# Slot attention and an FP8-weight FFN on one core: unsplit float32 products in the whole first unit, and other places for the norm blocks' transposes

## The chip, the cores and the metric

The kernel runs on one core of a Trainium2 chip. The metric is the device time of one execution in microseconds, here the median of three runs. The core's engines run their own instruction streams side by side and wait for each other by semaphores: PE (TensorE, matrix products and transposes), DVE (VectorE), ACT (ScalarE), POOL (GpSimd), and SP, which issues most DMAs.

## The reference, cut to what matters

Four sequences of 512 tokens with 512 features go through two residual blocks:

```python
x = x + attn(layernorm(x), Wq, Wk, Wv, Wg, Ws, Wo, g_norm_weight)
x = x + ffn(layernorm(x), gate_w, up_w, down_w, gate_scale, up_scale, down_scale)

# attn, 16 heads, DK = M = 64, DV = 128
q, k, v = heads(x @ Wq) * DK**-0.5, heads(x @ Wk), heads(x @ Wv)
s = clip(heads(x @ Ws), -32, 32)
z = cumlogsumexp(s); p = exp(s - z); g = exp(z_before - z)
hk = hk * g + k * p;  ok = q . hk          # over time
pv = softmax(ok)
hv = hv * g + p * v;  o = pv . hv          # over time
o = o * rsqrt(mean(o**2) + eps) * g_norm_weight * silu(x @ Wg)
return o @ Wo

# ffn: weights rounded to float8_e4m3, silu(gate) * up, then down
```

The two recurrences are computed in blocks of 128 tokens: products inside a block under a triangular mask, and states summed over the earlier blocks.

## The kernel before, in words

**Units.** `attention(g, b, before, load)` handles two heads (group g of 8) of one sequence b. The 32 units run in the order (0,0), (0,1), (1,0), (1,1) ... (7,1), then the same with b = 2, 3 (L1013); the text counts them as unit 0 to unit 31. A unit with even g projects values for two groups. Each unit also finishes the one before it (`before`): scaling, turning, gating and projecting its output. After the units comes the FFN over the four sequences in 12 chunks of the hidden size (L1076 on).

**Split products.** PE multiplies float32 operands that were prepared as float32r. A matrix or an activation is split into three parts, hi, lo and a mixed one (L238 to L250 for weights, `parts` L336 for activations: two DVE instructions and one of ACT). A projection is then eight products into one PSUM buffer ("main", four hi, then four lo) and four into another ("mixed"); ACT evacuates the first and DVE subtracts the second (L469 to L489, values L510 to L526). The PSUM pool `proj` has three buffers. In unit 0, the projections s, k and q take unsplit operands (L492 to L503): four products of float32 with `raw` weights and with `whole`, the unsplit norm of sequence 0, which lies in a buffer of tag "v".

**Order.** The schedule is written out by hand: each engine executes in the order in which the code emits (L998). Side work stands in a list `work` of named entries. `other()` takes `pace` entries from its front and emits them, `need(key)` takes entries from the front until none of that name is left. `pace` is 2 in a unit that starts with entries in `steps`, else 1 (L1054). `load_matrix(nm, g, True)` queues the split of a weight matrix: one entry for the first hi piece on ACT, then for each piece of 512 columns an entry with the next hi on ACT and two DVE instructions ("rest"), which at a matrix's end also issues the copy of the split to DRAM on SP; s, k and q have one piece, g and o two, v four. Raw weights come through two buffers; `fetch()` issues the next raw load once a buffer's split is done. In the first 16 units the matrices are split, in the later 16 units the splits are read back from DRAM and `work` holds the rounding of the FFN weights ("round", entries of two DVE instructions).

**Norm blocks.** `layernorm(b, which)` queues for sequence b four `measure` entries (three DVE instructions and a power on POOL) and the first `normalise` entries. It returns a function that puts four entries into `steps`; `next_step()` emits one: four PE transposes of a block of 128 tokens into a PSUM bank (one of three in turn), ACT's copy of the hi part, and a queue entry "xs_b" with the block's `parts`. The bank is `held`: the next use of it emits these parts first. Norms are transposed in unit 0 (for b=1), unit 15 (for b=2), unit 16 (for b=3), unit 31 (for the FFN of b=0) and in the FFN.

**A unit's order on PE.** Slots s, keys k, queries q, turns of e and k; values in four blocks (even g) with the previous unit's output turned between them, or that output's turn alone (odd g); query_key (a), the two gates, slot_scores (ok), value_states (sv), softmax (okn), the previous unit's output projection o in four blocks, slot_weights (w), weight_slot (b), read_out (ov). `softmax` on DVE is a maximum and a subtraction; `softmax_exp` is on ACT.

Of the kernel before, what the change touches and what calls it, by code (L numbers as in the profile page):

```python
# [37 lines left out]
F32 = mybir.dt.float32  # L38
# [6 lines left out]
P = 128  # L45
# [4 lines left out]
def kernel(  # L50
# [116 lines left out]
    def other(count=None):  # L167
        for _ in range(count or pace[0]):
            if work:
                work.pop(0)[1]()  # L170

    def need(key):

        while any(name == key for name, _ in work):
            other(1)
# [46 lines left out]

    def load_matrix(nm, g, first):
        words = CHUNKS[nm] * MATRICES[nm][1]
        w = one.tile([P, 3, words], F32R, tag=f"w_{nm}", name=f"w_{nm}_{g}")
        wt[nm] = w
        if not first:
            nc.sync.dma_start(w.bitcast(F32), split[nm, g])
            return
        scale = QSCALE if nm == "q" else 1.0  # L230
        pieces = words // 512

        def source(n):

            per = min(pieces, RAW // 512)
            return raw[nm, g][n // per][:, n % per * 512 : (n % per + 1) * 512]

        def high(n):  # L238
            nc.scalar.mul(w[:, 0, n * 512 : (n + 1) * 512], source(n), UNDER * scale)

        def rest(n):
            cols = slice(n * 512, (n + 1) * 512)
            hi, lo = w[:, 0, cols].bitcast(F32), w[:, 1, cols].bitcast(F32)
            if scale == 1.0:
                nc.vector.tensor_tensor(w[:, 1, cols], source(n), hi, ALU.subtract)  # L245
            else:
                nc.vector.scalar_tensor_tensor(
                    w[:, 1, cols], source(n), scale, hi, ALU.mult, ALU.subtract
                )
            nc.vector.scalar_tensor_tensor(w[:, 2, cols], hi, DELTA, lo, ALU.mult, ALU.subtract)  # L250
            if (n + 1) * 512 % RAW == 0 or n + 1 == pieces:
                if g > 0 or nm in "vo":
                    fetch()
            if n + 1 == pieces:
                split[nm, g] = dram.tile(
                    [P, 3, words], F32, tag=f"split_{nm}_{g}", name=f"split_{nm}_{g}"
                )
                nc.sync.dma_start(split[nm, g], w.bitcast(F32))

        def step(n):  # L260

            if n + 1 < pieces:
                high(n + 1)
            rest(n)

        work.append((nm, lambda: high(0)))
        work.extend((nm, lambda n=n: step(n)) for n in range(pieces))
# [21 lines left out]
    def layernorm(b, which, n_bank=None):  # L289
# [59 lines left out]
        if start:  # L349
            for n in range(NT):  # L350
                measure(n)
                if n > 0:
                    normalise(n - 1)
                    transposes(n - 1)
            normalise(NT - 1)
            transposes(NT - 1)
            work.extend((f"xs_{b}", lambda n=n: parts(n)) for n in range(NT))
            return None
        key = f"xn{which}_{b}_"
        todo = [(key + "m", lambda n=n: measure(n)) for n in range(NT)]  # L360
        todo.insert(2, (key + "0", lambda: normalise(0)))
        todo.insert(4, (key + "1", lambda: normalise(1)))
        at = max([i + 1 for i, (name, _) in enumerate(work) if name in ("xs_0", "v", "g")], default=0)
        work[at:at] = todo

        def step(n):
# [96 lines left out]
    class Projection:  # L463
# [5 lines left out]
        def main(self, to):  # L469
# [8 lines left out]
            self.to = to  # L478
            nc.scalar.mul(to, self.p, 1.0 + DELTA)  # L479

        def mixed(self):

            self.m = ps3.tile([P, T], F32, tag="proj", name=f"ps_{self.name}_m")
            for c in range(KC):
                nc.tensor.matmul(  # L485
                    self.m, products(self.nm, c, self.col0, 2), xs[self.b][2][:, c, :],
                    start=(c == 0), stop=(c == KC - 1),
                )
            nc.vector.tensor_tensor(self.to, self.to, self.m, ALU.subtract)  # L489

    def project(nm, b, name, to, between=None):
        if name == f"{nm}_0_0":  # L492
            p = ps3.tile([P, T], F32, tag="proj", name=f"ps_{name}")
            for c in range(KC):
                nc.tensor.matmul(
                    p, raw[nm, 0][0][:, c * P : (c + 1) * P], whole[0][:, c, :],
                    start=(c == 0), stop=(c == KC - 1),
                )
            other({"s": NT + 2, "k": 1, "q": 3}[nm])
            nc.scalar.mul(to, p, QSCALE if nm == "q" else 1.0)  # L500
            if between:
                between()
            return  # L503
        p = Projection(nm, b, 0, name)
        p.main(to)
        if between:
            between()
        p.mixed()

    def project_v(b, n, name, to):  # L510

        p = ps3.tile([P, 2 * HV], F32, tag="proj", name=f"ps_{name}")
        m = ps3.tile([P, 2 * HV], F32, tag="proj", name=f"ps_{name}_m")
        for dst, which in ((p, (0, 1)), (m, (2,))):
            for i in which:
                for c in range(KC):
                    nc.tensor.matmul(  # L517
                        dst,
                        xs[b][i][:, c, n * P : (n + 1) * P],
                        wt["v"][:, i, c * 2 * HV : (c + 1) * 2 * HV],  # L520
                        start=(i == which[0] and c == 0),
                        stop=(i == which[-1] and c == KC - 1),
                    )
            if dst is p:
                nc.scalar.mul(to, p, 1.0 + DELTA)  # L525
        nc.vector.tensor_tensor(to, to, m, ALU.subtract)  # L526
# [48 lines left out]
    class Heads:  # L575
# [168 lines left out]
        def gate_main(self, h):  # L744
            self.sg.append(one.tile([P, T], F32, tag=f"sg{h}", name=f"sg_{self.u}_{h}"))
            self.pg = Projection("g", self.b, h * DV, f"g_{self.u}_{h}")
            self.pg.main(self.sg[h])

        def gate_mixed(self, h):
            self.pg.mixed()  # L750
# [54 lines left out]
    def attention(g, b, before, load):  # L805
# [7 lines left out]
                before.project_output(n)  # L813
                before.add_output(n)

        if b or g:
            need(f"xs_{b}")
            need("s")
        X.slots()
        load("s")  # L820
        if before:
            before.scale_output()
        if b or g:
            need("k")

        def running_sum():
# [4 lines left out]

        X.keys(running_sum)
        load("k")
        if b or g:
            need("q")
        X.queries(other if even and before else None)
        load("q")
        X.turn_e()
        if even:
            X.turn_k()  # L840
            need(f"xs_{b}")
            need("v")
            X.values(0)
            if before:
                before.turn_output(0)
# [1 line left out]
            X.inverse()  # L847
            X.values(1)
            other()
            if before:  # L850
                before.high_output(0)
                before.split_output(0)
                before.turn_output(1)
# [6 lines left out]
            next_step()  # L860
            X.values(3)
            other()
        else:
            before.turn_output(0)
            X.turn_k()
# [5 lines left out]
            before.split_output(0)  # L871
            before.split_output(1)
            X.inverse()
            next_step()
        need("g")
        X.gate_main(0)
        X.gate_mixed(0)
        if even or steps:
            other()
            next_step()  # L880
        X.gate_main(1)
        X.gate_mixed(1)
        load("g")
        if even:
            load("v")
        X.gate_silu(0)
        X.gate_silu(1)
        exp_and_log()
        X.slot_scores()
        X.value_states()  # L890
        if even:
            other()
        if before:
            next_step()
        X.softmax()
        if not before:
            next_step()
        if not even:
            other()
        if before:  # L900
            need("o")
            before.project_output(0)
# [1 line left out]
        if before:  # L904
            before.add_output(0)
            before.project_output(1)
        X.slot_weights()
        if before:
            before.add_output(1)
# [88 lines left out]
    with tc.manual_schedule(engines=EVERY):  # L998
# [3 lines left out]
            (nc.scalar if n % 2 else nc.sync).dma_start(x1[0][:, n, :], blocks[:, n, :])  # L1002
        exp_and_log()
        fetch_first()
        layernorm(0, 1)
        for nm in "vgskqo":
            load_matrix(nm, 0, True)
        load_tokens(1, x)
        for b in range(2):
# [6 lines left out]
        for i, (g, b) in enumerate(units):  # L1016
            last = i + 1 == len(units)

            def load(nm):
                after = (i + 1 + 2 * (nm == "v")) // 2 * 2  # L1020
                if b == B - 1 and after == len(units):
                    for c, tag in enumerate(PLACES):
                        if tag == f"w_{nm}":
# [46 lines left out]
                load_ffn(c)  # L1070

        assert not work and not steps
        before.scale_output()
        before.scale_other()
        prev, kept = None, []
        for b in range(B):  # L1076
            need(f"xs_{b}")
            for c in range(NFC):
                if c > 1:
                    other(2)  # L1080
                h = ffn_hidden(b, c)
                if b == 0 and 0 < c < 3:
                    before.turn_output(c - 1, 2)
                    before.high_output(c - 1)
                    before.split_output(c - 1)
# [2 lines left out]
                    before.add_output(c - 3)  # L1088
                if c == 1 and b + 1 < B:
                    load_tokens(b + 1, stream, *((two, "v"), (one, "tokens"), (one, "y"))[b])  # L1090
                    layernorm(b + 1, 2, 2)()
                if prev is not None:
                    pb, pc, parts = prev
# [56 lines left out]
```

## Time and profile before

| | |
|---|---|
| median of 3 runs (lowest, highest) | 1534.4 us (1533.82, 1536.49) |
| the profiled execution, its span | 1534.67 us, 1532.9 us |
| mean granted TensorE clock | 0.991 |
| busy: PE, PEld | 1466.4 us (96%), 1182.0 us (77%) |
| busy: DVE, ACT, POOL | 1112.2 us (73%), 705.8 us (46%), 191.1 us (12%) |
| moved by DMA | 212.53 MB, mean 139 GB/s |

PE is the matrix engine's product stream, PEld its weight loads, which run beside it. Busy time is the time in which an engine executes an instruction; the rest it waits or is issued nothing. In timelines a row is: start in us from the span's start, duration in us, engine, line, operation, written tile <- read tiles, shapes, count, and in brackets the idle time before it and what ended it. The first groups of the page for the unsplit products (line 495), in us busy and mean ns of one record:

```profile
L495 PE MATMUL ps_s<-xn_whole,raw_sk 128*128 128x512 f32 x8 | 6.1, 938 | 0.7 <-ACT xn_whole L329 0.7
L495 PE MATMUL ps_k<-xn_whole,raw_sk 128*128 128x512 f32 x8 | 3.6, 592 | 0.0
L495 PE MATMUL ps_q<-xn_whole,raw_q 128*128 128x512 f32 x8 | 3.6, 592 | 0.0
```

Each has eight records for the four products of the code. The first of them ran at the clock of the start, before the full clock was granted at 17.9 us.

### The profile page before, as it was taken

The page shows a single profiled execution, that of the slowest core. Times are in us where ns is not written, and L with a number is a line of the kernel's source. Part 1 is how long each engine was busy: PE and PEld are TensorE (multiplying, and loading weights), DVE is VectorE, ACT ScalarE, POOL GpSimd, SP SyncE. Part 2 cuts the span into 40 slices and gives each one's busy share as a digit, 9 for nine tenths or more (in the row PEclk, how much of TensorE's full clock was granted, in tenths as well). Part 3 has the DMA queues.
Part 4 walks back from the last instruction along what each step waited for, and adds up shares of the span by engine and source line. Part 5 has one row for each costly group of instructions (what it writes and reads, how often), then busy time and mean ns, then how long its engine had stood idle before and what let it go on. Part 6 is the DMA issues. An engine that isn't in the chain of part 4 may idle for free.

```text
span 1532.9 us, 23073 instructions
## 1 busy us (share of the span) xinstructions
PE 1466.4 (96%) x9077; PEld 1182.0 (77%) x9077; DVE 1112.2 (73%) x1974; ACT 705.8 (46%) x1214; POOL 191.1 (12%) x204
## 2 busy tenths in 40 slices
PE   7799899999999999889999999999999989999998
PEld 4678688778877888677777778777777768787886
DVE  7678767877888788777888888888888754445333
ACT  4455445564565555444554454445444543222221
POOL 1011110111111111110111111111111111000000
PEclk9899999999999999999999999999999999999999
DMA  8146545575555564436564746575565452101000
GB/s 311 67 137 180 178 111 164 167 221 153 144 187 183 151 220 131 103 68 224 123 185 104 246 109 175 137 231 138 156 183 168 133 162 28 55 1 56 0 28 28
DMA packets 80716, 212.53 MB, mean 139 GB/s; under 512 B 6152, under 2 KB 34848, under 8 KB 75424
## 3 DMA queue, kind: packets, MB, share of 16 engines
q1 hardware_dynamic: 61792, 176.96, 31.6%
q0 software_dynamic: 18528, 33.58, 15.5%
q8 instruction: 71, 1.16, 0.3%
q10 hardware_dynamic: 288, 0.52, 0.1%
q14 instruction: 37, 0.30, 0.1%
HBM read 107.23 MB, written 108.00 MB: 140 GB/s over the span
## 4 chain that ended last, share of the span: by engine, by line
PE 78%; DVE 14%; ACT 4%; issue 2%; DMA 1%; POOL 0%; SPq 0%; DVEq 0%; ACTq 0%; POOLq 0%
PE ps_v L517 8%; PE ps_o L784 7%; PE ps_fu L929 5%; PE ps_fg L929 4%; PE ps_g L474 4%; PE ps_ov L714 4%; PE ps_v_m L517 4%; PE ps_o_m L784 3%; PE ps_q L474 3%; PE ps_g_m L485 3%; PE ps_s L474 3%; PE ps_k L474 3%; PE ps_b L544 2%; PE ps_a L544 2%; PE ps_fd L973 2%; PE ps_fe L973 2%
## 5 line engine op out<-in xcount | busy, mean ns | idle before, releaser
L800 POOL DMA_DIRECT2D stream<-y x128 | 110.9, 869 | 921.2 <-DVE y L799 916.2
L784 PE MATMUL ps_o<-w_o,oT 128*128 128x512 f32 x512 | 151.2, 416 | 2.3 <-DVE w_o L245 2.1
L794 ACT ACTIVATE y<-ps_o 128x512 f32<-128x512 f32 x128 | 76.3, 596 | 126.5 <-PE ps_o L784 125.4
L517 PE MATMUL ps_v<-w_v,xs 128*128 128x512 f32 x512 | 132.9, 401 | 0.0
L474 PE MATMUL ps_g<-xs,w_g 128*128 128x512 f32 x512 | 129.1, 394 | 0.0
L950 DVE SCALAR_TENSOR_TENSOR h<-ps_fu,scol,act 128x512 f32<-128x512 f32 x48 | 36.0, 750 | 105.2 <-PE ps_fu L929 102.6
L474 PEld LDWEIGHTS ps_g<-xs,w_g 128*128 128x128 f32 x512 | 94.6, 188 | 20.7
L517 PEld LDWEIGHTS ps_v<-w_v,xs 128*128 128x128 f32 x512 | 92.3, 188 | 20.4
L784 PEld LDWEIGHTS ps_o<-w_o,oT 128*128 128x128 f32 x512 | 90.5, 191 | 21.8 <-DVE w_o L245 2.7
L774 ACT ACTIVATE oT<-oT 128x512 fp32r<-128x512 f32 x64 | 40.5, 633 | 133.1 <-DVE oT L771 133.1
L799 DVE TENSOR_TENSOR y<-y,ps_o_m 128x512 f32<-128x512 f32 x128 | 87.2, 681 | 16.4 <-ACT y L794 8.0
L929 PE MATMUL ps_fg<-xs,wf 128*128 128x512 f32 x384 | 97.1, 395 | 0.0
L929 PE MATMUL ps_fu<-xs,wf 128*128 128x512 f32 x384 | 95.1, 390 | 1.2 <-ACT act L947 1.2
L929 PEld LDWEIGHTS ps_fu<-xs,wf 128*128 128x128 f32 x384 | 72.0, 188 | 16.7 <-ACT act L947 1.6
L784 PE MATMUL ps_o_m<-w_o,oT 128*128 128x512 f32 x256 | 81.4, 399 | 1.8 <-ACT y L794 1.7
L929 PEld LDWEIGHTS ps_fg<-xs,wf 128*128 128x128 f32 x384 | 71.7, 189 | 14.7
L526 DVE TENSOR_TENSOR v<-v,ps_v_m 128x512 f32<-128x512 f32 x64 | 43.9, 685 | 47.5 <-PE ps_v_m L517 41.4
L956 ACT CAST both<-h 128x512 fp32r<-128x512 f32 x48 | 29.8, 620 | 105.2 <-DVE h L950 105.2
L485 PE MATMUL ps_g_m<-xs,w_g 128*128 128x512 f32 x256 | 70.6, 398 | 4.3 <-ACT sg L479 4.3
L489 DVE TENSOR_TENSOR sg<-sg,ps_g_m 128x512 f32<-128x512 f32 x64 | 43.9, 686 | 41.6 <-PE ps_g_m L485 38.2
L525 ACT ACTIVATE v<-ps_v 128x512 f32<-128x512 f32 x64 | 37.9, 592 | 76.6 <-PE ps_v L517 76.6
L729 POOL TENSOR_TENSOR rs<-rs,mhalf 128x8 f32<-128x8 f32 x32 | 58.6, 1830 | 87.5 <-DVE rs L726 82.1
(159 smaller groups left out, 3218.3 us busy)
## 6 DMA issues: line engine op xcount, KB each, us to landing
stream<-y POOLq DMA_DIRECT2D x128, 256.0 KB, 5.3
split_v<-w_v SPq DMA_DIRECT2D x4, 3072.0 KB, 12.0
split_g<-w_g SPq DMA_DIRECT2D x8, 1536.0 KB, 8.2
split_o<-w_o SPq DMA_DIRECT2D x8, 1536.0 KB, 6.1
w_v<-split_v SPq DMA_DIRECT2D x4, 3072.0 KB, 15.2
w_g<-split_g SPq DMA_DIRECT2D x8, 1536.0 KB, 6.7
w_o<-split_o SPq DMA_DIRECT2D x8, 1536.0 KB, 9.5
rounded<-qw SPq DMA_DIRECT2D x36, 256.0 KB, 4.1
```

The lines of the kernel that those rows point to most:

```text
L474: nc.tensor.matmul(self.p, products(self.nm, c, self.col0, i), xs[self.b][i][:, c, :], start=(i == 0 and c == 0), stop=(i == 1 and c == KC ...
L485: nc.tensor.matmul(self.m, products(self.nm, c, self.col0, 2), xs[self.b][2][:, c, :], start=(c == 0), stop=(c == KC - 1),)
L517: nc.tensor.matmul(dst, xs[b][i][:, c, n * P : (n + 1) * P], wt["v"][:, i, c * 2 * HV : (c + 1) * 2 * HV], start=(i == which[0] and c == 0 ...
L544: nc.tensor.matmul(pa[h][:, n, :], lT[rows, cols], rT[rows, cols], start=True, stop=True)
L714: nc.tensor.matmul(po[h][:, n, :], self.bb[h][:, n, :], both_v[self.b][:, n, self.v0 + h * DV : self.v0 + (h + 1) * DV], start=False, stop ...
L729: nc.gpsimd.tensor_tensor(rs, rs, mhalf.rearrange("p (h n) -> p h n", h=HG), ALU.pow)
L784: nc.tensor.matmul(dst, self.oT[:, i, h, n * P : (n + 1) * P], wt["o"][:, i, h * D : (h + 1) * D], start=(i == which[0] and h == 0), stop= ...
L794: nc.scalar.mul(y, p, 1.0 + DELTA)
L799: nc.vector.tensor_tensor(y, y, m, ALU.subtract)
L800: nc.gpsimd.dma_start(stream[self.b][n * P : (n + 1) * P, :], y, accum_op=ALU.add)
L929: nc.tensor.matmul(pp, w[:, c * P : (c + 1) * P], xs[b][k][:, c, :], start=(c == 0 and k == 0), stop=(c == KC - 1 and k == 1),)
L973: nc.tensor.matmul(sums[n], parts[k][:, n * P : (n + 1) * P], fw[c][2], start=(c == 0 and k == 0), stop=(c == NFC - 1 and k == 1),)
```

## The change

In unit 0 all projections take unsplit operands: values from `whole` and the raw v pieces, gates from the raw g. The two gates move from before slot_scores to both sides of softmax. The splits of v, g and o of group 0, and the four `parts` of sequence 0's norm, are queued late in unit 0 instead of at the start; s, k and q are split first. The split tile `w` is allocated when its first piece is emitted. In all units with a predecessor, `other()` of even g moves from before softmax to behind it, where odd g has it. Where `steps` holds norm blocks, their transposes are emitted at other places: in odd units after slots and after keys (`early_step`), in even units after values 1, 2 and 3 and between the gates. The measures of a later norm are queued behind "v", "g" and "q" entries instead of "xs_0", "v" and "g". In the FFN the last unit's output is scaled after the first hidden block, and the next sequence's norm is queued at chunk 2 instead of 1.

```diff
     def load_matrix(nm, g, first):
         words = CHUNKS[nm] * MATRICES[nm][1]
-        w = one.tile([P, 3, words], F32R, tag=f"w_{nm}", name=f"w_{nm}_{g}")
-        wt[nm] = w
+
+        def begin():
+            wt[nm] = one.tile([P, 3, words], F32R, tag=f"w_{nm}", name=f"w_{nm}_{g}")
+
         if not first:
-            nc.sync.dma_start(w.bitcast(F32), split[nm, g])
+            begin()
+            nc.sync.dma_start(wt[nm].bitcast(F32), split[nm, g])
             return
...
         def high(n):
+            if n == 0:
+                begin()
+            w = wt[nm]
...
-            work.extend((f"xs_{b}", lambda n=n: parts(n)) for n in range(NT))
-            return None
+            return [(f"xs_{b}", lambda n=n: parts(n)) for n in range(NT)]
...
-        at = max([i + 1 for i, (name, _) in enumerate(work) if name in ("xs_0", "v", "g")], default=0)
+        at = max([i + 1 for i, (name, _) in enumerate(work) if name in ("v", "g", "q")], default=0)
...
+        def whole(self):
+
+            p = ps3.tile([P, T], F32, tag="proj", name=f"ps_{self.name}")
+            width = MATRICES[self.nm][1]
+            for c in range(KC):
+                at = c * width + self.col0
+                nc.tensor.matmul(
+                    p, raw[self.nm, 0][0][:, at : at + P], whole[0][:, c, :],
+                    start=(c == 0), stop=(c == KC - 1),
+                )
+            return p
...
-            other({"s": NT + 2, "k": 1, "q": 3}[nm])
+            p = Projection(nm, b, 0, name).whole()
+            other({"s": 6, "k": 2, "q": 2}[nm])
...
+        if name == f"v_0_0_{n}":
+            p = ps3.tile([P, 2 * HV], F32, tag="proj", name=f"ps_{name}")
+            for c in range(KC):
+                w = raw["v", 0][c // 2].rearrange("p (c n) -> p c n", c=2)
+                nc.tensor.matmul(
+                    p, whole[0][:, c, n * P : (n + 1) * P], w[:, c % 2, :],
+                    start=(c == 0), stop=(c == KC - 1),
+                )
+            nc.scalar.copy(to, p)
+            return
...
-            self.pg.main(self.sg[h])
+            if self.u == "0_0":
+                nc.scalar.copy(self.sg[h], self.pg.whole())
+            else:
+                self.pg.main(self.sg[h])
...
-        if b or g:
+        def early_step():
+
+            if not any(name.endswith("_m") for name, _ in work):
+                next_step()
+
+        if before:
             need(f"xs_{b}")
             need("s")
         X.slots()
         load("s")
+        if not even:
+            early_step()
         if before:
             before.scale_output()
-        if b or g:
             need("k")
...
         load("k")
-        if b or g:
+        if not even:
+            early_step()
+        if before:
             need("q")
-        X.queries(other if even and before else None)
+        X.queries(other if before and (even or steps) else None)
         load("q")
         X.turn_e()
         if even:
             X.turn_k()
-            need(f"xs_{b}")
-            need("v")
+            if before:
+                need(f"xs_{b}")
+                need("v")
+                need("xs_0")
             X.values(0)
...
             X.values(1)
             other()
+            next_step()
...
             X.values(3)
             other()
+            next_step()
...
             X.inverse()
-            next_step()
-        need("g")
-        X.gate_main(0)
-        X.gate_mixed(0)
-        if even or steps:
-            other()
-            next_step()
-        X.gate_main(1)
-        X.gate_mixed(1)
-        load("g")
-        if even:
-            load("v")
-        X.gate_silu(0)
-        X.gate_silu(1)
-        exp_and_log()
+        if before:
+            need("g")
+            X.gate_main(0)
+            X.gate_mixed(0)
+            if even:
+                other()
+                next_step()
+            X.gate_main(1)
+            X.gate_mixed(1)
+            load("g")
+            if even:
+                load("v")
+            X.gate_silu(0)
+            X.gate_silu(1)
+            exp_and_log()
         X.slot_scores()
         X.value_states()
-        if even:
-            other()
-        if before:
-            next_step()
-        X.softmax()
         if not before:
             next_step()
-        if not even:
-            other()
+            X.gate_main(0)
+        X.softmax()
+        other()
         if before:
             need("o")
             before.project_output(0)
...
             before.project_output(1)
+        else:
+            X.gate_main(1)
+            X.gate_silu(0)
+            X.gate_silu(1)
+            exp_and_log()
+            load("v")
+            load("g")
         X.slot_weights()
...
-        layernorm(0, 1)
-        for nm in "vgskqo":
+        parts_0 = layernorm(0, 1)
+        for nm in "skq":
             load_matrix(nm, 0, True)
...
             def load(nm):
                 after = (i + 1 + 2 * (nm == "v")) // 2 * 2
+                if i == 0:
+                    if nm in "vgo":
+                        load_matrix(nm, 0, True)
+                    if nm == "v":
+                        work.extend(parts_0)
+                    return
...
-        before.scale_output()
-        before.scale_other()
...
                 h = ffn_hidden(b, c)
+                if b == 0 and c == 0:
+                    before.scale_output()
+                    before.scale_other()
...
                     load_tokens(b + 1, stream, *((two, "v"), (one, "tokens"), (one, "y"))[b])
+                if c == 2 and b + 1 < B:
                     layernorm(b + 1, 2, 2)()
```

More of the change, by code (lines that the diff above doesn't have):

```diff
@@ L238, in high @@
         def high(n):
+            if n == 0:
+                begin()
+            w = wt[nm]
             nc.scalar.mul(w[:, 0, n * 512 : (n + 1) * 512], source(n), UNDER * scale)
         def rest(n):
+            w = wt[nm]
             cols = slice(n * 512, (n + 1) * 512)
@@ L492, in project @@
         if name == f"{nm}_0_0":
[L493 to L498, printed above, removed]
-            other({"s": NT + 2, "k": 1, "q": 3}[nm])
+            p = Projection(nm, b, 0, name).whole()
+            other({"s": 6, "k": 2, "q": 2}[nm])
             nc.scalar.mul(to, p, QSCALE if nm == "q" else 1.0)
```

## The prediction

> **What bounds the kernel now.** I read the engine shares first, then the chain by engine:
>
> ```profile
> PE   7799899999999999889999999999999989999998
> ...
> PE 78%; DVE 14%; ACT 4%; issue 2%; DMA 1%; POOL 0%; SPq 0%; DVEq 0%; ACTq 0%; POOLq 0%
> ```
>
> PE works nearly everywhere, so the change is worth what it adds to PE or takes from PE's gaps. To find the gaps I cut the timeline at the first ps_s product of each of the 32 units (unit i is the i-th (g, b)). Plain odd-g units take 31.7 us (2, 6, 10, 14). Even ones take 41.8 (8, 12), in the second half 42.8 (b=2) and 42.5 (b=3). Dear ones: unit 0 53.7, 1 45.7, 3 37.6, 4 44.6, 15 41.7, 16 48.1, 31 38.6. Then PE's waits in units 1, 3 and 4 (waiter, releaser, us, times, longest):
>
> ```profile
> PE ps_s L474 <- ACT xs L347: 2.4, 1, 2.4
> ...
> PE ps_q L474 <- ACT w_q L239: 2.5, 1, 2.5
> PE ps_o L784 <- DVE w_o L245: 2.1, 2, 1.3
> ```
>
> These are late splits: unit 1 waits for its norm's last block, unit 4 for w_q, unit 3 for w_o. Then the clock, by 3.4 us stretches (length; busy PE, PEld, DVE, ACT, POOL; granted clock):
>
> ```profile
> 52.03:55.44 3.41, 0.63 (x4) 0.42 (x4) 2.70 (x5) 1.73 (x3) 0.00 (x0) 1.00 0.00 0
> 55.44:58.85 3.41, 1.91 (x6) 1.22 (x6) 2.11 (x5) 0.02 (x1) 0.00 (x0) 0.50 0.00 0
> 58.85:62.27 3.42, 3.37 (x20) 2.85 (x22) 2.31 (x4) 1.91 (x4) 0.00 (x0) 0.50 0.02 5
> 62.27:65.68 3.41, 3.41 (x22) 3.19 (x21) 0.90 (x2) 0.42 (x2) 0.00 (x0) 0.50 0.49 202
> ...
> 168.08:171.49 3.41, 1.64 (x5) 0.85 (x6) 2.87 (x5) 0.60 (x2) 0.00 (x0) 1.00 0.02 5
> 171.49:174.90 3.41, 3.41 (x12) 2.72 (x11) 0.69 (x1) 1.11 (x2) 0.89 (x1) 0.50 1.03 396
> 621.90:625.30 3.40, 1.72 (x9) 0.99 (x8) 2.12 (x4) 1.93 (x5) 0.00 (x0) 1.00 0.00 0
> ```
>
> A stretch with PE under about half busy (1.64, not 1.72) is followed by half clock: 1.7 us lost per stretch full of work.
>
> **The change, in the queue's order.** I followed `work`, `steps` and `held` by hand through both versions.
>
> *Units 0 and 1.* Plain products: k and q at full clock took 3.43 us each in the chain for four products, a split projection 1.83+0.92=2.75. Four values and two gates: PE +4.1 us. (The Trainium skill, "FP8 and Floating Point Precision", TensorE Precision Notes, speaks against this: true FP32 is four passes. At 2.75/12 per split product that makes 3.67 and +5.5. The row decides: +4.1.) PE to q ends at 25.95 as now, e and k turns at 26.8. Then values 13.7, key states and a 1.6, norm turns 1.8, ok and sv 2.6, gates 6.9, okn and w 1.2, b 1.1, ov 2.85, and waits of 0.9 (exp) and 0.8 (wT): unit 1 starts at 60.2 instead of 66.7, without its 2.4 wait. A lead of 8.9.
> But all v, g, o splits and the four xs_0 parts now come after unit 0's softmax. ACT first does two table loads (1.28 each) and two silus (1.15): first v high at 59.7. DVE then: three v splits (1.38 each) to 63.9, rs sums and scol 1.7, the fourth v split and an xs_0 part 2.8, then the eT subtraction to 69.0. Only that frees the third proj buffer for q; PE has finished k at 65.7. So q starts at 69.1 (now 74.9); another part ahead of kT's subtraction puts v0 at 74.2 (now 78.45): lead 4.2. The g split just ahead of the gate costs 0.4. Then both o splits stand behind softmax, exactly as in unit 3, which takes 15.5 from okn (166.19) to its end against 11.6 in unit 1 now; 1.7 of the 3.9 is clock. I take 3.1. Units 0+1: **-0.7** (ends -8.9, everything hidden, and +3). DMAs: three 768 KB copies of s, k, q move to 15-18 us, behind x1, which landed at 16.1 and is first read at 20; raw_o and raw_s go from 20.9 and 25.6 to over 60, landing takes 3 to 3.5, first use some 35 us later: nothing.
>
> *Unit 2.* k1 and q1 now come where unit 4 has k2 and q2: +2.6 (unit 4's excess is 2.8). `need("g")` forces both g splits directly ahead of gate_main(0). Now:
>
> ```profile
> 124.58 2.12 PE L474 MATMUL ps_g<-xs,w_g 128*128 128x512 f32 x8
> ...
> 127.81 0.69 DVE L771 SCALAR_TENSOR_TENSOR oT<-oT 128x512 fp32r<-128x512 f32 x1
> 128.41 0.69 DVE L616 SCALAR_TENSOR_TENSOR z<-z,rzT 128x512 f32<-128x512 f32 x1
> 128.53 0.64 ACT L774 ACTIVATE oT<-oT 128x512 fp32r<-128x512 f32 x1 [0.70 <-DVE oT L771]
> 129.13 0.69 DVE L617 SCALAR_TENSOR_TENSOR rzT<-z,rzT 128x512 f32<-128x512 f32 x1
> ```
>
> PE reaches the gates 5.2 us before DVE has done a, splits and inverse (129.8). The g highs stand behind L774 on ACT (129.2), the g splits on DVE behind L617: 129.8+4x0.69=132.5. The mixed products end at 133.0 instead of 127.4; 0.5 comes back in the next gate: +5.1. PE idles 5 us, so one half-clock stretch, +1.3. (The skill's "TensorE: Matmul & The Clock Gate", What's actually happening, asks for a whole idle window of 3.4 us. 5 us idle holds one about half the time, so +0.7; the stretch at 168.08, cut with 1.64 busy, contradicts it, and I keep 1.3.) Unit 2: **+9.0** (ends +4 and +11).
>
> *`other()` behind softmax in even units.* Only units 17, 20, 21, 24, 25, 28, 29 have DVE work there (a rounding step, 1.4 or 1.1 us). Now w waits 0.8 for exp. Moved, it stands ahead of the first add_output, which frees the buffer of the third ps_o; from okn b starts at 5.8 instead of 6.2. 0.4x7: **-2.8** (0 to -6).
>
> *Unit 15.* Two turns go early, where PE has them for their 0.44 each; their parts delay sg on DVE by 1.9 and PE by 1.0. The three stalls (2.3, 1.7, 2.7) and one half-clock stretch go. o7's last split lands behind softmax: half of unit 3's price, 2.2. 31.7+1.8+1.0+2.2=36.7: **-5.0** (-7 to -3). But the last turn now stands ahead of read_out, its parts in the next unit.
>
> *Unit 16.* layernorm(3,1) puts its measures ahead of these parts ("xs_2" is not among "v", "g", "q"), and need("xs_2") runs all:
>
> ```profile
> 637.31 2.08 PE L474 MATMUL ps_s<-xs,w_s 128*128 128x512 f32 x8
> ...
> 639.03 0.69 DVE L312 BATCH_NORM_STATS2 stats<-x 128x6 f32<-128x512 f32 x1
> 639.29 1.92 POOL L729 TENSOR_TENSOR rs<-rs,mhalf 128x8 f32<-128x8 f32 x1
> ...
> 640.94 1.30 POOL L315 TENSOR_TENSOR rstd<-rstd,mhalf 128x1 f32<-128x1 f32 x2
> ```
>
> Behind two measures (to 641.1) come the wait for the first power (641.6), norm 0.54, measure 1.0, norm 0.54, measure 1.0, parts 1.38, ACT 0.63: 646.7. ps_s has its four hi products by 638.2, and its lo products wait: +8.3 (unit 1 had one part there, 2.4), and 1.5 stretches at half clock, +2.5. All of PE's queue waits behind it. After values(1) the first block's bank is asked for again by query_key, so its parts (1.38) follow split and sg (2.1) in front of a: +3.3. Softmax loses its stalls (48.1-41.8-1.8=4.5), but parts of block 3 with ACT's multiply now stand ahead of exp, as in unit 15 now (w 5.2 after okn instead of 3.2): -4.5+2.0. Sum **+11.6** (+3 to +16).
>
> *Unit 31 and FFN.* As unit 15 without o: 31.7+1.8 against 38.6, -5.1. The last parts (0.69) move behind rs: the second ps_fg product waits until 1247.2 instead of 1244.9, +2.3. scale_output behind the first hidden block frees ACT for silu: ps_fu's 1.2 goes. **-4.0** (-6 to -1). Later norms starting at c=2: six queue entries at two per block are done by c=5, before the turns: 0.
>
> **Sum.** -0.7+9.0-2.8-5.0+11.6-4.0=+8.1. The profiled execution took 1534.67 (span 1532.9, 1.8 around it), 0.3 above the median: 1542.8 by it, 1542.5 against the median. I say 1542.5.
>
> **Rivals.** (a) *VectorE absorbs the deferred splits*, not slower: for it speaks that DVE is 73% busy; against it, that in unit 3 and 4 the same order made PE wait. Place: units 0 to 2; price: the lead of 8.9 kept and unit 2 unchanged, 17.2 less, 1525.3. It decides once over 8.1 of these 17.2 is regained. 0.15. (b) *Unit 16's parts come in time*, because the measures find slack under unit 15's tail: 10.8 less, 1531.7; against it, the order is fixed and DVE starts them after rs. 0.12. (c) *The clock stays down* three stretches after each new stall, as from 55.44: about 6 more, 1548.5. 0.2. (d) That the change doesn't do all it says: in units 15 and 31 only two of four turns come between projections, the others stay at the end; that is in the forecast. Forecast: 0.53.
>
> A measurement tells 0.2% (3 us) from no change. Faster: most of (a) and half of (b), 0.18; same: the rest of these and a tail of the forecast, 0.12; slower 0.70. The range 1530 to 1553 leaves out most of (a) and the extremes of (c) with unit 2's and 16's upper ends.
>
> **What would show it.** Right: ps_s of unit 1 near 60 and its ps_q waiting for eT; ps_g of unit 2 waiting some 5 us for w_g; ps_s of unit 16 waiting some 8 us for xs L347; half clock after both; unit 15 near 37 us, unit 31 near 33.5. Wrong: unit 2 below 34 us, unit 16 below 50, or a lead over 5 us at unit 2's start.

## The result, and the profile after

The changed kernel takes **1542.8 us** (median of 5 runs, 1541.0 to 1543.0), the one before on the same chip 1534.6 us (5 runs, 1533.8 to 1536.5): a ratio of 1.0047, 95% interval 1.0032 to 1.0062. By the medians the change costs 8 us; the interval of the ratio makes it 5 to 10. The profiled execution took 1541.84 us with a span of 1540.0 us (before: 1534.67 and 1532.9) and a mean granted clock of 0.987 (before: 0.991).

The granted clock and the chain by engine, from the page of the changed kernel:

```profile
PEclk9998999999999999989999999999999999999999
...
PE 81%; DVE 13%; ACT 4%; issue 2%; DMA 0%; POOL 0%; DVEq 0%; POOLq 0%; ACTq 0%
```

PE still carries the chain, so the account is again one of PE's stalls, unit by unit. Each unit is cut at its first ps_s product, as in the prediction; lengths in us:

| unit | before | after | forecast of the difference | measured |
|---|---|---|---|---|
| 0, 1 | 53.73, 45.74 | 46.81, 53.67 | -0.7 | +0.9 at unit 2's start |
| 2 | 31.64 | 42.66 | +9.0 | +11.0 |
| 15 | 41.67 | 37.35 | -5.0 | -4.3 |
| 16 | 48.10 | 62.93 | +11.6 | +14.8 |
| 17, 20, 24, 28 | 42.82 | 41.83 | -0.4 each | -1.0 each |
| 21, 25, 29 | 42.54 | 41.83 | -0.4 each | -0.7 each |
| 31 and FFN | 38.58 + 288.23 | 34.17 + 283.23 | -4.0 | -9.4 |
| span | 1532.9 | 1540.0 | +8.1 | +7.1 |

All other units agree within 0.05 us. PE's waits in unit 1, in unit 2 and in unit 16 of the changed kernel (waiter, releaser, us in all, times, longest):

```profile
PE ps_k_m L503 <- ACT eT L485: 3.9, 1, 3.9
PE ps_o L810 <- DVE w_o L252: 1.6, 2, 0.8
...
PE ps_g L480 <- ACT w_g L245: 5.1, 1, 5.1
PE ps_q L480 <- ACT w_q L245: 2.5, 1, 2.5
...
PE ps_s L480 <- ACT xs L354: 8.5, 1, 8.5
PE ps_a L567 <- DVE xs L349: 3.2, 1, 3.2
PE ps_o_m L810 <- ACT y L820: 1.7, 1, 1.7
```

The last six stand where the forecast had them. Those for w_g, w_q, xs and in front of a have nearly its sizes (5.1, 2.6, 8.3 and 3.3), ps_o had been given more (3.1), and the wait for y makes the 5.2 from okn to w that the forecast took over from unit 15. The first is not the forecast one: in unit 1 it is the mixed product of k that waits, not q. The timeline there (columns as before):

```profile
66.55 0.69 DVE L351 SCALAR_TENSOR_TENSOR xs<-xs,xs 128x512 fp32r<-128x512 f32 x1
67.28 0.63 ACT L354 ACTIVATE xs<-xs 128x512 fp32r<-128x512 f32 x1 [5.75 <-DVE xs L351]
67.81 0.58 ACT L485 ACTIVATE eT<-ps_s 128x512 f32<-128x512 f32 x1
68.44 2.07 PE L503 MATMUL ps_k_m<-xs,w_k 128*128 128x512 f32 x4 [3.91 <-ACT eT L485]
```

L485 reads the slots' PSUM buffer, and the products of k's mixed part need that buffer. It could run as soon as PE had ended ps_s, but an xs_0 part's multiply stands ahead of it on ACT, which waits 5.75 us for DVE. ACT runs in order, so the wait of one instruction became PE's wait.

In unit 2 the chain to the gates is the forecast one. The hi parts of w_g are made on ACT and stand there behind the multiply of oT, which waits for DVE:

```profile
133.86 0.63 ACT L800 ACTIVATE oT<-oT 128x512 fp32r<-128x512 f32 x1 [0.70 <-DVE oT L797]
134.40 1.14 ACT L245 ACTIVATE w_g<-raw_g 128x512 fp32r<-128x512 f32 x2
...
135.07 1.65 PE L480 MATMUL ps_g<-xs,w_g 128*128 128x512 f32 x3 [5.09 <-ACT w_g L245]
```

In unit 16 all four measures of the new norm and two normalisations run on DVE ahead of the parts that the slots' lo products need:

```profile
646.68 0.69 DVE L319 BATCH_NORM_STATS2 stats<-x 128x6 f32<-128x512 f32 x1
...
651.47 0.69 DVE L319 BATCH_NORM_STATS2 stats<-x 128x6 f32<-128x512 f32 x1
...
652.48 0.68 DVE L349 TENSOR_TENSOR xs<-ps_xn,xs 128x512 fp32r<-128x512 f32 x1
653.19 0.69 DVE L351 SCALAR_TENSOR_TENSOR xs<-xs,xs 128x512 fp32r<-128x512 f32 x1
653.92 0.63 ACT L354 ACTIVATE xs<-xs 128x512 fp32r<-128x512 f32 x1 [8.07 <-DVE xs L351]
...
654.60 2.08 PE L480 MATMUL ps_s<-xs,w_s 128*128 128x512 f32 x4 [8.46 <-ACT xs L354]
```

What the stall leaves behind is seen in the clock (stretch, length, busy PE, PEld, DVE, ACT and POOL with counts, granted clock, DMA share, GB/s):

```profile
648.11:651.53 3.42, 0.00 (x0) 0.00 (x0) 2.60 (x9) 0.00 (x0) 2.37 (x4) 0.50 0.41 77
651.53:654.94 3.41, 0.34 (x1) 0.34 (x2) 2.25 (x6) 0.63 (x1) 0.61 (x2) 0.50 0.01 2
654.94:658.36 3.42, 3.42 (x9) 2.65 (x9) 0.00 (x0) 0.60 (x1) 0.00 (x0) 0.50 0.00 0
...
672.01:675.42 3.41, 0.69 (x5) 0.33 (x3) 2.55 (x5) 1.62 (x3) 0.00 (x0) 1.00 0.00 0
675.42:678.83 3.41, 2.98 (x16) 2.61 (x17) 2.27 (x4) 0.63 (x1) 0.00 (x0) 0.50 0.00 0
678.83:682.25 3.42, 3.42 (x9) 2.64 (x8) 0.00 (x1) 0.60 (x2) 0.00 (x0) 0.50 0.00 0
```

At half clock a stretch full of work does about half of it: 9 products in the one from 654.94, 17 in the next at full clock. The 8.5 us stall therefore cost a further (0.34 + 3.42)/2 = 1.9, and the second one, 3.2 us in front of a, a further (2.98 + 3.42)/2 = 3.2. The prediction had 2.5 for the first and nothing for the second.

### The profile page after: what moved, and what is told of

It is laid out like the page before. It is cut to its first block, busy times and chain, and to the rows that moved or that the text cites. A ratio compares the mean times of both kernels' runs of the same rounds, so it can differ in the third digit from the quotient of the medians.

```text
span 1540.0 us, 23008 instructions
## 1 busy us (share of the span) xinstructions
PE 1471.5 (96%) x9053; PEld 1180.2 (77%) x9053; DVE 1109.0 (72%) x1968; ACT 708.3 (46%) x1214; POOL 193.0 (13%) x204
## 4 chain that ended last, share of the span: by engine, by line
PE 81%; DVE 13%; ACT 4%; issue 2%; DMA 0%; POOL 0%; DVEq 0%; POOLq 0%; ACTq 0%
PE ps_o L810 8%; PE ps_v L540 7%; PE ps_fg L970 5%; PE ps_fu L970 5%; PE ps_ov L737 4%; PE ps_o_m L810 4%; PE ps_g L480 4%; PE ps_v_m L540 3%; PE ps_q L480 3%; PE ps_g_m L503 3%; PE ps_s L480 3%; PE ps_k L480 3%; PE ps_fd L1014 2%; PE ps_a L567 2%; PE ps_fe L1014 2%; PE ps_b L567 2%
## 5 line engine op out<-in xcount | busy, mean ns | idle before, releaser
L540 PE MATMUL ps_v<-w_v,xs 128*128 128x512 f32 x480 | 126.2, 405 | 0.0
L540 PEld LDWEIGHTS ps_v<-w_v,xs 128*128 128x128 f32 x480 | 87.6, 190 | 19.6 <-issue 0.2
L480 PE MATMUL ps_s<-xs,w_s 128*128 128x512 f32 x248 | 66.1, 408 | 8.5 <-ACT xs L354 8.5
```

What stands on the lines that cost most here:

```text
L480: nc.tensor.matmul(self.p, products(self.nm, c, self.col0, i), xs[self.b][i][:, c, :], start=(i == 0 and c == 0), stop=(i == 1 and c == KC ...
L540: nc.tensor.matmul(dst, xs[b][i][:, c, n * P : (n + 1) * P], wt["v"][:, i, c * 2 * HV : (c + 1) * 2 * HV], start=(i == which[0] and c == 0 ...
```

## The experiments

Three questions were open: is each gain and loss the one named; what is the stall itself and what is the clock; and is it the plain products of the first unit that cost the time, or the places to which its deferred splits went? All ratios are to the kernel before, run beside each experiment. The reference point for "less" and "more" is the change at 1542.8 us.

**The order of parts and measures (unit 16).** The measures are queued behind the parts that are still waiting:

```diff
-        at = max([... if name in ("v", "g", "q")], default=0)
+        at = max([... if name in ("v", "g", "q") or name.startswith("xs_")], default=0)
```

> The change, with the measures of a later norm queued behind waiting 'xs' entries. Theory (queue order at the start of unit 16): ps_s of unit 16 waits 2.5 to 3 us for its norm's last block instead of 8.5, the half clock after it goes or shrinks, unit 16 takes 53 to 55 us instead of 62.9, the whole 8 to 10 us less than the change (about 1534). Rival (the cost of unit 16 lies in where the transposes stand, the banks and softmax): unit 16 stays above 59 us, the whole less than 3 us shorter.

1535.48 us, ratio 1.0006 (0.9998 to 1.0014): 7.3 us less than the change. Unit 16 went from 62.93 to 56.60. Its waits:

```profile
PE ps_a L567 <- DVE xs L349: 3.2, 1, 3.2
PE ps_s L480 <- ACT xs L354: 2.7, 1, 2.7
```

The wait of the slots fell from 8.5 to 2.7, not far above the 2.0 that one part's two DVE and one ACT instruction take; the wait in front of a stayed. So the queue order is the mechanism; unit 16 stayed above the 53 to 55 expected, and the gain below the 8 to 10. One condition in one line is worth nearly the whole loss, which leaves this kernel level with the one before.

**The clock's share of that stall.** The measures stay in front, so DVE is as late as in the change, but PE is given 36 spare products to run between the hi and the lo products of the slots. Their results are overwritten:

```diff
+                if i == 0 and self.name == "s_0_2":
+                    self.m = ps3.tile([P, T], F32, tag="proj", ...)
+                    for _ in range(36):
+                        nc.tensor.matmul(self.m, products(...), xs[...], start=True, stop=True)
```

> The change, with 36 spare products (8.2 us at full clock, their result is overwritten) between the hi and the lo products of ps_s in unit 16, where PE otherwise waits. Theory (the wait costs a second time through the clock): the wait stays, but the full clock is granted behind it; unit 16 takes 60 to 61 us instead of 62.9, the whole 2 to 3 us less. Rival (the half clock there is hidden behind VectorE anyway): unit 16 stays at 62.9 or longer.

1539.09 us, 1.0031 (1.0019 to 1.0042). Unit 16 took 59.83, 3.1 less than in the change:

```profile
646.54 8.34 PE L487 MATMUL ps_s_m<-xs,w_s 128*128 128x512 f32 x36
655.16 1.20 PE L480 MATMUL ps_s<-xs,w_s 128*128 128x512 f32 x4 [0.28 <-ACT xs L354]
```

The lo products start no earlier within the unit (9.64 us after its first ps_s product in both kernels); they only run at full clock: four of them in 1.20, where the change took 2.08. The half clock around 648 is gone; after a's stall one half-clock stretch is left (from 676.3) instead of two. Work that computes nothing made the kernel 3.7 us faster (median against median), which separates the two prices of a stall: here 8.5 for the wait and, of the 3.1, 1.7 for the clock behind it up to a's stall. The other 1.4 comes from behind a's stall, where the stretches fall differently here and leave only one at half clock.

**`other()` in even units, put back** in front of softmax:

```diff
+        if before and even:
+            other()
         X.softmax()
-        other()
+        if not (before and even):
+            other()
```

> The change, with other() of even units ahead of softmax again. Theory by the unit lengths of the changed kernel: units 17, 20, 24, 28 get 1.0 us back each and 21, 25, 29 0.7 each, the whole 6 us longer than the change (about 1548.8). Rival (the price of the forecast, 0.4 each): 2.8 us longer, and something else shortened these units. Unit 1 may shift by up to 1 us either way.

1546.43 us, 1.0075 (1.0061 to 1.0089). Units 17, 20, 24 and 28 are back at 42.81, units 21, 25 and 29 at 42.53, as before the change. PE's rows behind okn in unit 20 here, and then the same in the changed kernel:

```profile
844.90 0.66 PE L557 MATMUL ps_okn<-ident,okT 128*128 128x128 f32 x4
...
849.12 0.66 PE L557 MATMUL ps_w<-ident,ok 128*128 128x128 f32 x4 [0.83 <-ACT ok L697]
849.54 1.17 PE L810 MATMUL ps_o<-w_o,oT 128*128 128x512 f32 x4
...
851.09 1.16 PE L567 MATMUL ps_b<-wT,eT 64*128 64x128 f32 x16
```

```profile
844.37 0.65 PE L557 MATMUL ps_okn<-ident,okT 128*128 128x128 f32 x4
...
847.60 0.60 PE L557 MATMUL ps_w<-ident,ok 128*128 128x128 f32 x4
847.99 1.20 PE L810 MATMUL ps_o<-w_o,oT 128*128 128x512 f32 x4
...
849.58 1.16 PE L567 MATMUL ps_b<-wT,eT 64*128 64x128 f32 x16
```

From okn to b it is 6.2 with the rounding step in front of softmax and 5.2 behind it. The move is worth 1.0 in four units and 0.7 in three, 6.0 in all by the unit lengths; the two spans differ by 5.5, with a shift of 0.75 the other way in unit 16. The medians differ by only 3.6, nearer the rival's 2.8, because the profiled execution is below its median in the change and above it here, each by 0.9. The verdict rests on the units, which agree with the theory one by one.

**The FFN's later norms, put back** to the chunk where they were:

```diff
-                if c == 2 and b + 1 < B:
+                if c == 1 and b + 1 < B:
                     layernorm(b + 1, 2, 2)()
```

> The change, with the next sequence's norm queued at chunk 1 of the FFN again. Theory (the first measure waits for the DMA of x at the head of VectorE's queue and holds h behind it): chunks 3 and 4 of the second and third sequence get longer by 4.1 and 1.1 us, the whole 5.2 us longer than the change (about 1548). Rival (the FFN is shorter because the scaling of the last output moved): no more than 1 us longer.

1549.06 us, 1.0091 (1.0077 to 1.0104). The FFN takes 290.86 instead of 283.23: +5.2 in one chunk of the second sequence, +0.5 in the one behind it, +1.3 in one of the third and +0.6 in the first sequence. That is 7.6 in all, and 6.3 by the medians, where 5.2 were expected. The timeline of the second sequence:

```profile
1351.54 0.69 DVE L319 BATCH_NORM_STATS2 stats<-x 128x6 f32<-128x512 f32 x1 [6.98 <-DMA x<-stream]
...
1353.57 0.75 DVE L991 SCALAR_TENSOR_TENSOR h<-ps_fu,scol,act 128x512 f32<-128x512 f32 x1
...
1355.03 0.50 PE L1014 MATMUL ps_fe<-wf,both 128*128 128x512 f32 x1 [3.34 <-ACT both L997]
```

A measure stands at the head of DVE and waits 7.0 us for the load of the next sequence's tokens; the hidden block h behind it needs no such data, yet it waits too, and through it PE. In the kernel before the same rows read:

```profile
1337.53 0.69 DVE L312 BATCH_NORM_STATS2 stats<-x 128x6 f32<-128x512 f32 x1 [5.32 <-DMA x<-stream]
...
1341.01 0.50 PE L973 MATMUL ps_fe<-wf,both 128*128 128x512 f32 x1 [1.71 <-ACT both L956]
```

At chunk 2 the load has nearly landed (the measure waits 1.9) and no PE product waits for it.

**The first unit alone.** The kernel before with only the first unit's changes: plain products for v and g, the new places of the splits, and the gates around softmax. Everything else of the change is undone but the place of a norm's measures in the queue, which shows no effect here (unit 16 takes 48.08, before 48.10).

> The kernel before with the change's first unit alone: unsplit products, its order and its queue; everything else stands where it stood. Theory (the deferred splits come due in units 1 and 2): unit 1 starts 6.9 us earlier, unit 2 ends some 12 us later than before, the rest as before, the whole about 12 us longer than before (1546.5). Rival (the loss needs the other moves too): less than 6 us longer. Second rival (the lead is kept): shorter than before.

1547.59 us, 1.0083 (1.0069 to 1.0096). Units 0 to 2 take 46.85, 53.39 and 42.84, as in the whole change; units 15, 16 and 31 and the FFN are within 1 us of before. So the first unit's part alone costs 13 us and all the rest together gives some 5 back.

**More splits per place in unit 1.** `pace` is 2 instead of 1 in that unit alone:

```diff
-            pace[0] = 2 if steps else 1
+            pace[0] = 2 if steps or i == 1 else 1
```

> The change, with two queue entries instead of one taken at each place of unit 1. Theory (unit 2 pays for entries that unit 1 left in the queue): the g, o, k and q splits run before unit 2 needs them; unit 2 returns to 31.7 us from 42.7, its waits of ps_q (2.5) and ps_g (5.1) go, unit 1 loses its ps_o waits and changes by -3 to +2; the whole 10 to 14 us less than the change (about 1530). Rival (VectorE has no room for them in unit 1): unit 1 grows by what unit 2 saves, the whole within 3 us of the change.

1524.9 us, 0.9941 (0.9929 to 0.9954): 17.9 less than the change. Units 1 to 4 take 52.09, 34.55, 32.68 and 41.78. Unit 2's waits for w_g and w_q are gone, and so are 4.95 in unit 3 and 2.85 in unit 4, which the expectation had not counted: these units drag the same queue. Unit 2 still stays 2.9 above the expected 31.7; ps_k_m waits 1.2 there. Of unit 1's waits the first stays: ps_k_m's longest is 3.9 as before.

**No queue entries at unit 1's start.** The two single `other(1)` between the units are left out for unit 1, so that no part stands in front of eT's evacuation:

```diff
-            if before:
+            if before and i != 1:
                 other(1)
```

> The change, without the two queue entries (a v split, a part of xs_0) that are taken at the start of unit 1; they come later in the same unit. Theory (ScalarE evacuates ps_s only behind the multiply of that part, in order, and PE's ps_k_m needs the buffer): the wait of ps_k_m (3.9 us) goes and with it the half clock at 68; as much as 2 us of it comes back before values, where the parts must be done; unit 1 takes 50 to 52.5 us instead of 53.7, the whole 1 to 4 us less than the change. Rival (VectorE as a whole is behind): unit 1 stays within 1 us of 53.7.

1539.24 us, 1.003 (1.0019 to 1.0042). The ps_k_m wait is gone and with it the half clock at 68 us: the releaser read off the timeline is the right one. But unit 1 only falls from 53.67 to 52.82, above the 50 to 52.5 expected and within the 1 us that the rival named: the entries come later and PE waits at other places (ps_kn for kT 1.4, v 0.7, w_g 1.5 for 0.8, w_o 2.3 as before), with two half-clock stretches from 100.3. Removing the stall moved most of it on; the queue as a whole was late.

**The old first unit with the rest of the change.** The kernel before, plus all the change outside the first unit, with three places mended: the measures behind waiting parts (as in the first experiment), the first turn of an even unit behind query_key, and waiting parts emitted ahead of read_out:

```diff
+        for name in [n for n, _ in work if n.startswith("xs_")]:
+            need(name)
         X.read_out()
```

> The kernel before with its own first unit, and the rest of the change with three places mended: measures behind waiting 'xs' entries, waiting 'xs' entries taken before read_out, in even units the first transpose behind query_key instead of before it. Theory (every loss of the change is a wait at a named place): unit 1 43 to 44 us, unit 2 31.7, the seven even units 41.8, unit 15 37, unit 16 45 to 47, unit 31 34, FFN 281; the whole 1505 to 1512. Rival (the early transposes cost what they save): above 1520.

1509.19 us (1508.22 to 1510.87), 0.9836 (0.9823 to 0.985). Units 0 to 4 take 52.56, 41.78, 32.67, 35.18 and 46.15. Unit 16 took 50.21, not the 45 to 47 expected: 1.7 for y, 1.3 for sg and 1.1 for xn remain in front of PE. The FFN took 280.85, 2.4 less than in the change, because its second product no longer waits for parts. Unit 3 still waits 1.5 for w_o and unit 4 2.5 for w_q.

**The new first unit with the same mending**, and pace 2 in unit 1:

> The change with all its parts, with the three places mended as in the run with the old first unit, and two queue entries at each place of unit 1. Theory: units 0 to 2 take 130 us or less against 131 in the kernel before, the rest as in the run with the old first unit, the whole 1503 to 1510, and the two runs within 5 us of each other. Rival (the deferred splits can't be placed without loss): units 0 to 2 take 136 us or more.

1515.99 us, 0.9878 (0.9863 to 0.9893). Units 0 to 2 sum to 140.3, so the rival's case came true: asking for the parts ahead of read_out pulled all the v splits in front of them into unit 0's end, and ps_k_m waits 8.4 in unit 1 and 2.7 in unit 2. To settle it, the same with that request only in units with a predecessor, and without the entries at unit 1's start:

```diff
+        if before:
+            for name in [n for n, _ in work if n.startswith("xs_")]:
+                need(name)
...
-            pace[0] = 2 if steps else 1
-            if before:
+            pace[0] = 2 if steps or i == 1 else 1
+            if before and i != 1:
                 other(1)
```

> As the mended version with the new first unit, but waiting 'xs' entries are taken before read_out only in units with a predecessor (unit 0 had taken all v splits and xs_0 parts there), and no entries at the start of unit 1. Theory: ps_k_m's wait (8.4 us) goes, units 0 to 2 take 127 to 132 us instead of 140.3, the whole 1503 to 1509. Rival (the new first unit costs more than the old one wherever its splits stand): units 0 to 2 above 132 us, the whole above that of the version with the old first unit (1509.2).

**1506.36 us** (1505.92 to 1507.9), 0.9818 (0.9805 to 0.9831): the fastest here, 28 us below the kernel before. Its page:

```profile
span 1504.6 us, 23008 instructions
...
PE 1459.2 (97%) x9053; PEld 1172.7 (78%) x9053; DVE 1106.2 (74%) x1968; ACT 706.3 (47%) x1214; POOL 192.0 (13%) x204
```

Units 0 to 4 take 46.75, 46.70, 36.65, 31.62 and 43.39, in sum 205.1; before 213.4, in the change 225.4, with the old first unit and the same three places mended 208.3. By the medians it is 2.8 us below that kernel (which ran on another chip; the kernel before took 1534.4 there and 1534.1 here). So the plain products can be carried at no loss against the kernel before, once the splits that they defer are placed. Whether they gain anything is open, because these two kernels differ in more than the first unit: pace 2 and the missing entries in unit 1 are in this one alone. Units 0 to 2 take 130.1 here and 127.0 there; the lead comes from units 3 and 4 (75.0 against 81.3), whose waits for w_o and w_q pace_2 had already removed from the change. The old first unit at pace 2 was not run.

PE does as many instructions as in the change and is busy 12.3 us less, at a mean clock of 0.997 for 0.987. What remains is of the kind already met, in unit 2:

```profile
113.05 0.63 ACT L245 ACTIVATE w_v<-raw_v 128x512 fp32r<-128x512 f32 x1 [5.82 <-DMA raw_v<-in_L_attn_Wv_dram]
113.58 0.58 ACT L485 ACTIVATE eT<-ps_s 128x512 f32<-128x512 f32 x1
...
114.22 1.20 PE L503 MATMUL ps_k_m<-xs,w_k 128*128 128x512 f32 x4 [3.04 <-ACT eT L485]
```

A weight's split at ACT's head waits for its load, and eT's evacuation waits behind it.

## Why the prediction was right, and where it was not

The median was forecast to within 0.3 us, but part of that is luck: the steps' errors, +1.6 in units 0 and 1, +2.0 in unit 2, +0.7 in unit 15, +3.2 in unit 16, -3.2 in the even units and -5.4 at the end, add up to -1.1 in the span.

**Units 0 and 1: near in sum (+0.9 for -0.7), wrong in one link.** Unit 1 starts at 59.7, forecast 60.2: the plain products cost what their rows said. "Only that frees the third proj buffer for q" failed: the buffer before it, the one that eT's evacuation on ACT frees for ps_k_m, was late already, because ACT stood behind a part's multiply. ps_k_m started at 68.4 and q at 70.3 instead of 69.1; with half clock from 67.9 to 74.7, which the forecast did not have, v0 came at 75.9 instead of 74.2, a lead of 2.6, not 4.2. The gate waits took 0.8 for 0.4, the o splits 2.3 for 3.1. unit1_no_pops shows the link, and that mending it alone gives little.

**Unit 2: right in both waits** (2.5 and 5.1, forecast 2.6 and 5.1). The term of the clock was too small: 1.3 was taken for one stretch, the trace has one after q's wait (122.5) and two after the gates' (132.7 to 139.5). The first and the last of these were full of work, so each cost 1.7. pace_2 shows that both waits come from the late queue.

**Even units: the gain's size failed.** "From okn b starts at 5.8 instead of 6.2": it was 5.2. The forecast made the third ps_o wait for the first add_output, which the moved step delays. That addition did come late (DVE began it at 847.78), but the third ps_o began at 847.99 directly behind w, and no row shows a wait. even_other_back gives the price as 1.0 and 0.7 by the unit lengths.

**Unit 15:** 4.3 gained for 5.0, with 1.5 and 1.1 waits for w_o and oT where one o split was foreseen.

**Unit 16: right in its causes.** The waits were 8.5 (forecast 8.3) and 3.2 (3.3). The excess of 3.2 is mostly clock: 5.1 by the stretches above for 2.5 forecast. parts_first and clock_kept show order and clock apart.

**The clock's rule failed outside the trace it was read from.** "A stretch with PE under about half busy (1.64, not 1.72) is followed by half clock" holds for the two rows named, but not in the changed kernel, as the last section shows; nor does the clock always return after one stretch, as the forecast took it to in unit 2.

**Unit 31 and the FFN: "Later norms starting at c=2: ... 0" failed.** Unit 31's gain (-4.4, forecast -5.1), the delay of the second ps_fg (its chunk +2.3, forecast +2.3) and the lost wait of ps_fu (its chunk -1.4, forecast -1.2) came nearly as worked out. But the prediction only asked whether six queue entries would be done in time by chunk 5. It did not look at what the first of them waits for in the kernel before, though its trace shows the 5.32 us on a DMA. Moving the norm by one chunk was worth 5.9 (0.6 in the first sequence, 3.5 and 0.6 in two chunks of the second, 1.1 in the third). ffn_norm_back lost 7.6 by undoing it, its wait for the load being longer, 7.0 for 5.3.

**The rivals.** (a) *VectorE absorbs the splits* did not happen in this form, though new_first_unit_mended_2 shows that DVE has the room: there units 0 to 2 take 130.1 against 131.1 before, with no more DVE instructions than the change. The lead of 8.9 was not reached in any run; the most at unit 2's start was 6.1. (b) *Unit 16's parts come in time* did not happen. (c) *The clock stays down* was half right: half clock lasted two or three stretches at four of the stalls, but the gains that the forecast had too small paid for it.

**Open.** Units 3 and 4 take 37.6 and 44.6 in some kernels and 36.0 and 46.2 in others, 82.2 in both. The half-clock stretch lies at 184 us in the changed kernel, one of the former, and at 201 in the latter, which would fit the phase of the stretches; no run separated it. The 1.7 that unit 16 waits for y was not tried.

## What to carry to other kernels

Deferring work in an in-order queue costs where it surfaces, not where it was: follow each deferred entry to the engine's head and ask what stands behind it, for here a part's multiply, a split and a statistic each stopped unrelated products. A stall can be priced twice, by its length and by the half-clock stretches behind it. Before a cost is written off as hidden, look in the old trace at what the first instruction of the moved step waits for.

## What the hardware showed that was not expected

Half clock can outlast a stretch that is nearly full of work. In unit 16 of the changed kernel the stretch from 675.42 held 2.98 us of work in 3.41, yet the full one behind it still ran at 0.50; in the kernel before the same followed a stretch with 3.37 (from 58.85). So a stall of 3.2 us cost as much again in clock. In parts_first, though, stretches with 2.83 and 2.88 (from 67.98 and 648.25) were enough for full clock. Every stretch filled with 3.41 brought it back.

The way down has no sharp line either, by the busy time that the profile counts. Three stretches of the changed kernel:

```profile
180.49:183.90 3.41, 2.06 (x7) 1.19 (x8) 2.69 (x5) 1.02 (x2) 0.00 (x0) 1.00 0.07 20
183.90:187.31 3.41, 3.41 (x12) 2.73 (x11) 1.13 (x3) 0.70 (x2) 0.89 (x1) 0.50 1.07 432
...
1255.68:1259.10 3.42, 1.57 (x13) 1.25 (x12) 2.07 (x4) 2.48 (x3) 0.36 (x1) 1.00 1.10 256
```

The first led to half clock with 2.06 us of work. The last held 1.57, and the clock stayed full: the next half clock comes at the program's end. In the kernel before, 1.64 led to half clock (168.08), and 1.72 and 1.97 (621.90 and 676.66) did not. What decides between 1.5 and 2.1 us stays open. That products of no use can pay (clock_kept, 3.1 us of unit 16) is the other side of this.
